# One order table for all engines in the window steps of a two-layer network: layer 0's steps rewritten, with transposes and attention a few steps later

## The chip, the core and the metric

The kernel runs on one core of one Trainium2 chip. The metric is the device time of one execution in microseconds, the median of three runs. The core has five instruction queues that run beside one another and meet at semaphores: TensorE (PE; its weight loads are shown as PEld), VectorE (DVE), ScalarE (ACT), GpSimd (POOL) and SyncE (SP), which here issues all the DMAs. Each queue executes in order: an instruction that waits holds up everything behind it on its own engine.

## The reference, cut to what matters

Sixteen images of 128 channels and 56 x 56 pixels go through two layers. The change is in layer 0 only, so layer 1 (a convolution, a state-space scan over eight tokens, a group norm) is left out here. Layer 0, for each image:

```python
x = x + dwconv3x3(x)                        # "position"
y = layernorm(x)
q, k, v = split(y @ qkv_w + qkv_b)          # 49 windows of 8 x 8 pixels
idx = top_k(mean(q) @ mean(k).T, 4)         # per window: the four windows it attends to
att = softmax(q * SCALE @ k[idx].T)         # 4 heads, 64 queries, 256 keys
o = att @ v[idx]
o = (o + dwconv5x5(v)) @ wo_w + wo_b        # "lepe"
x = x + o
x = x + gelu(layernorm(x) @ w1 + b1) @ w2 + b2
```

## The kernel before: tiles, steps and order

Channels lie on the 128 partitions. An image is seven rows of windows (`NBLK` = 7 blocks of `BLK` = 448 pixels), a row has seven windows (`WIN` = 7), so an image has 49 windows. The program is written image after image; `_chain` (L149) fixes, for each engine, the order in which the program wrote the instructions. So the order of the calls in the source *is* the order of each queue, and nothing else reorders it.

For each image, 49 calls of `step` (L618), then one call of `mlp` (L720). Step t handles window t of image `im`. It also carries two other pipelines in the gaps. One is the last row's output: `collect`, `project_out`, `residual`, and a layer norm `centred`, `squared`, `variance`, `logarithm`, `exponential`, `second`. The other is the next image's input, `nxt`: one row of `position`, a layer norm, `windows` (y and its window sums), `project` and `keep` for q, k and v. Over and above these run the 25 taps a row of the 5 x 5 convolution on DVE (`convolve_on`, L591, with the counts of `TAPS`), and on POOL the 3 x 3 convolution of the image after next or the next one (`beside_to`, L606).

A window goes through these functions:

- `gather` (L418, SP): four DMAs of 64 KB each bring the four chosen windows' keys and values from DRAM into a `sel` buffer, of which there are six. The gathers run `AHEAD` = 5 windows ahead. Every second window also loads its indices into SP's registers (L422).
- `scores` (L435, PE, eight matmuls at L441) into the one bank pair `ps`; `largest` (L445, DVE L447); `exponentials` (L449, ACT L453, two of them), after which `ps` is free for the next window; `inverse` (DVE L459) and `weights` (POOL L463, two multiplications).
- `transpose_values` (PE L471, for two windows at a time) into bank `pvt`, `keep_values` (ACT L478).
- `transpose_weights` (PE L485) into bank `ptt`, `keep_weights` (ACT L491), `attend` (PE L501) into bank `po`.

Bank `g0` serves the two layer norms' `centred` and the three `project`s in turn; `pvt` serves the transposed values, both `variance`s and `project_out`.

In `step`, scores, maximum, exponentials, inverse and weights are all of window t; the weights' transposes are of window t-1, the attention of window t-2 (in column 4 of a row none, in column 5 two). In column 5 the next image's row is squared and its logarithm taken, in column 6 come its exponential and `windows`, ahead of the last window's exponentials. `keep` of k and v writes to DRAM through SP (L390): two DMAs for k in column 1, behind the gather of window 7r+6, and one for v in column 2. Two loads of a later image's halves (L284) follow the gathers of windows 25 and 29.

`mlp` ends the image: it takes the remaining q, k, v of the next image's last row, loads ACT's table for gelu, does the last attentions, routes the next image (`sums`, `route`), issues that image's first five gathers, and runs seven blocks of the MLP, each with a store of `r` (L583). Before the change six of POOL's `beside` operations for the image after next are issued in steps 45 to 48, six more at the start of `mlp`, and the rest up to `LEAD` = 41 during it.

Of the kernel before, what the change touches and what calls it, by code (L numbers as in the profile page):

```python
# [10 lines left out]
F32 = mybir.dt.float32  # L11
# [6 lines left out]
P = 128  # L18
# [191 lines left out]
def layer0(ctx: ExitStack, tc: tile.TileContext, x, t, x1, conv):  # L210
# [117 lines left out]
        else:  # L328
            nc.gpsimd.tensor_add(im["xh"][i], im["xh"][i], held["tap"])  # L329

    def centred(at, im, i):
        held["pc"] = at[:, 0:BLK]
        nc.tensor.matmul(held["pc"], lhsT=centre, rhs=im["xh"][i], start=True, stop=True)

    def squared(n):
        sq = held["sq"] = w1.tile([P, BLK], F32, tag="sq", name=f"sq_{n}")
        nc.scalar.activation(sq, held["pc"], AF.Square)

    def variance(at):
        held["pv"] = at[:, 0:BLK]  # L340
        nc.tensor.matmul(held["pv"], lhsT=mean, rhs=held["sq"], start=True, stop=True)

    def logarithm(n):
        rstd = held["rstd"] = w1.tile([P, BLK], F32, tag="rstd", name=f"rstd_{n}")
        nc.scalar.activation(rstd, held["pv"], AF.Ln, bias=eps)

    def exponential():
        nc.scalar.activation(held["rstd"], held["rstd"], AF.Exp, scale=-0.5)

    def deviation(n):  # L350
        logarithm(n)
        exponential()

    by_row = "c (r w x) -> c w r x"

    def windows(im, i):

        n = f"{im['b']}_{i}"
        y = held["y"] = w1.tile([P, BLK], F32, tag="y1", name=f"y1_{n}")
        nc.vector.tensor_mul(  # L360
            y.rearrange("c (w r x) -> c w r x", w=WIN, r=8),
            held["pc"].rearrange(by_row, r=8, w=WIN),
            held["rstd"].rearrange(by_row, r=8, w=WIN),
        )
        if i == 0:
            im["sum"] = w2.tile([P, NW], F32, tag="ysum", name=f"ysum_{n}")
            im["val"] = w2.tile([P, NW, WP], F32, tag="val", name=f"val_{n}")
            im["dram"] = dram.tile([NW, P, 3, WP], F32, tag="dkv", name=f"dkv_{n}")
        nc.vector.tensor_reduce(
            im["sum"][:, WIN * i : WIN * i + WIN], y.rearrange("c (w p) -> c w p", p=WP), AX.X, ALU.add  # L370
        )
# [186 lines left out]
    def residual(im, r):  # L558
        xh = im["xh"][r]
        nc.vector.scalar_tensor_tensor(xh, held["pw"], wo_b, xh, ALU.add, ALU.add)  # L560

    def second(im, r):
        y2 = im["y2"][r] = w1.tile([P, BLK], F32, tag=f"y2{r}", name=f"y2_{im['b']}_{r}")
        nc.vector.tensor_mul(y2, held["pc"], held["rstd"])

# [16 lines left out]

    TAPS = ((2, 1), (2, 0), (2, 1), (2, 1), (2, 1), (2, 1), (1, 1))

    slot = [0]

# [9 lines left out]

    ROUND = NBLK * len(OPS)
    LEAD, FIRST = 41, 26
    ENDS = (9, 16, 23, 30, 37, 45)
    begun = [ROUND]

    def beside_to(n, count):  # L606
# [8 lines left out]
        scores(im, t)  # L615
        largest(im, t)

    def step(im, nxt, t):  # L618
        r, c = divmod(t, WIN)
        b = im["b"]  # L620
        n = f"{b}_{t}"
        out, row = (im, r - 1) if r else (images[b - 1], NBLK - 1)
        old, new = r > 0 or b > 0, nxt is not None
        if t + AHEAD < NW:
            gather(im, t + AHEAD)
        if t == 0 and early and not new:
            conv.load(0)
        if t in ((20, 24) if b else (30, 34, 38, 42)) and b + 2 < NB:
            load(b + 2, t // 4 - 5) if b else load(2, t // 4 % 2, t // 8 % 2)

        if c < 3 and new and r:
            keep(nxt, r - 1, c)
        if c == 2 and old:
            residual(out, row)
        if c == 3 and old:
            squared(n)
        if c == 6 and new:
            exponential()
        if c == 5 and new:
            squared(n)  # L640
        if t > 0 or b == 0:
            open_step(im, t)
        for w in {4: (), 5: (t - 3, t - 2)}.get(c, (t - 2,)):
            if w >= 0:
                attend(im, w)
        if c == 1 and r:
            collect(im, r - 1)
        if c == 4 and old:
            second(out, row)
        if c == 6 and new:  # L650
            windows(nxt, r)
        taps = TAPS[c] if t else (1, 2)
        convolve_on(taps[0])
        if new:
            lead = LEAD if b else FIRST
            if t in ENDS:
                position(nxt, 1 + ENDS.index(t), (8,))
            if t < 45:
                beside_to(b + 1, lead + -(-(ROUND - lead) * (t + 1) // 45))
            else:  # L660
                beside_to(b + 2, 3 * (t - 44) // 2)
        exponentials(im, t)
        inverse(im, t)
        if t in (3, 10, 17, 31):
            surround(im, 3 + (3, 10, 17, 31).index(t))
        if t in (38, 45) and new:
            surround(nxt, (t - 38) // 7)
        weights(im, t)
        if c == 1 and new and r:
            project(g0, 2)  # L670
        waits = c in (1, 4, 6)
        if not waits:
            piece(im, nxt, out, row, c, r)
        if c == 4:
            transpose_values(im, t)
        if t > 0:
            transpose_weights(im, t - 1)
            if c == 3 and old:
                deviation(n)
            keep_weights(im, t - 1)  # L680
        if c % 2 == 0:
            if c != 4:
                transpose_values(im, t)
            keep_values(im, t)
        if c == 5 and new:
            logarithm(n)
        convolve_on(taps[1])
        if waits:
            piece(im, nxt, out, row, c, r)

    def piece(im, nxt, out, row, c, r):

        old, new = r > 0 or im["b"] > 0, nxt is not None
        if c == 0 and new and r:
            project(g0, 1)
        if c == 1 and old:
            project_out(pvt)
        if early and not new:
            first(r if c > 4 else r - 1, {5: (0, 1, 2), 6: (3, 4), 0: (5, 6, 7), 1: (8,)}.get(c, ()))
        if c == 2 and old:  # L700
            centred(g0, out, row)
        if c == 3 and old:
            variance(pvt)
        if c == 4 and new:
            centred(g0, nxt, r)
        if c == 5 and new:
            variance(pvt)
        if c == 6 and new:
            project(g0, 0)

    early = NB > 2

# [65 lines left out]
    def norm_begun(i):  # L778

        centred((g0, ps[:, 0, :])[i % 2], im, i)  # L780
        means[i] = held["pc"]
        squared(f"0_{i}")


# [27 lines left out]
    begin(im, 4, nc.vector)  # L812
    position(im, 4, (1, 2))
    for i in range(NBLK):
        held["pc"] = means[i]
        windows(im, i)
        if i + 1 < NBLK:
            variance(ptt)
            deviation(f"0_{i + 1}")
# [27 lines left out]
        position(images[1], 0, (8,))  # L847
    for b in range(NB):
        im, nxt = images[b], images[b + 1] if b + 1 < NB else None
        for w in range(NW):  # L850
            step(im, nxt, w)
        mlp(im, nxt)
        if b:
            images[b - 1].clear()
    r = NBLK - 1
    project_out(pvt)
    residual(im, r)
    centred(g0, im, r)
    squared("end")
    variance(pvt)  # L860
    deviation("end")
    second(im, r)
    _act_set(tc, "gelu_and_others")
    for s in range(3):
# [562 lines left out]
```

## Time and profile before

| | us |
|---|---|
| median of three runs | 8227.22 (8224.33 to 8235.01) |
| the profiled execution's own time | 8228.15 |
| its span, first to last instruction | 8226.3 |
| PE busy in the span | 7775.7 (95%) |
| DVE busy | 7590.8 (92%) |
| POOL busy | 6994.9 (85%) |
| ACT busy | 5681.2 (69%) |
| first scores of image 0 | 86.8 |
| last scores of image 15 | 3030.3 |

The granted clock is 0.988 of full speed over the span and 1.00 in the steps of layer 0. The stretch of layer 0 is some 3 of the 8.2 ms; the rest is layer 1, whose instructions the change leaves as they are. An image's cycle, from one image's sixth gather to the next one's, takes 184 to 188 us in images 1 to 13. The 43 windows from window 5 to 48 take 130 to 132 us of it.

How to read it: a row "1098.72:1119.86" is a stretch of the span in microseconds, followed by its length and each engine's busy time in it with the number of instructions. In a list of waits, "DVE y L360 <- ACT rstd L348: 35.4, 87, 0.7" says that DVE's instruction of line 360 stood idle for what ACT did at line 348, 35.4 us in all, 87 times, 0.7 us at the longest. In a timeline the columns are the start, the length from the first to the last of a merged group, the engine, the line, the operation, the tile written from the tiles read, and the count.

### The profile page before, as it was taken

How to read it: one execution, taken by the hardware profiler on the slowest of the kernel's cores; microseconds unless marked ns; L12 is line 12 of the kernel's file. 1: busy time of each engine (PE TensorE's matmuls, PEld its weight loads, DVE VectorE, ACT ScalarE, POOL GpSimd, SP SyncE). 2: the span in 40 equal slices, each digit the busy share in tenths (PEclk: the TensorE clock that was granted, in tenths of full speed). 3: DMA queues.
4: the chain of work that ended last, by engine and by line, in shares of the span. 5: the costliest groups of instructions: out<-in, count | busy, mean ns of one | idle time of the engine just before them, and what ended most of it. 6: DMA issues, size and time to landing. Idle time of an engine off the chain costs nothing.

```text
span 8226.3 us, 155700 instructions
## 1 busy us (share of the span) xinstructions
PE 7775.7 (95%) x53380; PEld 3294.9 (40%) x53380; DVE 7590.8 (92%) x10105; ACT 5681.2 (69%) x10695; POOL 6994.9 (85%) x5569
## 2 busy tenths in 40 slices
PE   8899999999999988999999999999999999999998
PEld 4444444444444443333333333333333333333333
DVE  7999999999999958999999999999999999999998
ACT  5777777777777756666666766666766666666665
POOL 7888888888888627899999998989998989989997
PEclk9999999999999999999999999999999999999998
DMA  5544455554544423333434434333334333344333
GB/s 117 116 111 113 115 115 116 116 118 115 115 112 113 110 75 83 92 89 97 108 82 105 103 88 105 100 90 100 96 90 109 83 103 101 89 104 104 88 92 86
DMA packets 1072005, 835.24 MB, mean 102 GB/s; under 512 B 496112, under 2 KB 971376, under 8 KB 1069296
## 3 DMA queue, kind: packets, MB, share of 16 engines
q1 hardware_dynamic: 1071216, 825.28, 41.0%
q8 instruction: 427, 7.00, 0.4%
q14 instruction: 362, 2.97, 0.1%
HBM read 645.13 MB, written 179.83 MB: 100 GB/s over the span
## 4 chain that ended last, share of the span: by engine, by line
PE 52%; DVE 21%; POOL 11%; ACT 9%; issue 5%; DMA 1%; SPq 0%; DVEq 0%; ACTq 0%; POOLq 0%
PE a L1053 10%; PE pq L185 9%; PE pq L1099 5%; DVE h L1071 5%; POOL xh L329 4%; DVE a L1081 4%; PE x L1064 4%; DVE h L1086 3%; POOL tap L327 3%; PE pq L1133 3%; POOL e L463 2%; PE ptt L485 2%; PE pq L1105 2%; ACT e L453 2%; PE ps L441 2%
## 5 line engine op out<-in xcount | busy, mean ns | idle before, releaser
L1090 POOL TENSOR_TENSOR cst<-h,cb 128x1792 f32<-128x1792 f32 x784 | 3129.3, 3998 | 341.0 <-DVE h L1086 271.5
L1056 ACT ACTIVATE a<-a 128x896 f32<-128x896 f32 x1568 | 1415.9, 903 | 1191.2 <-PE x L1064 969.1
L1071 DVE TENSOR_TENSOR h<-x,bb 128x896 f32<-128x896 f32 x1568 | 1696.3, 1082 | 134.1 <-PE x L1064 100.0
L544 DVE SCALAR_TENSOR_TENSOR lepe<-vpad,lep,lepe 128x448 f32<-128x448 f32 x2688 | 1707.5, 677 | 0.5
L1053 PE MATMUL a<-dt,adec 32*128 32x448 f32 x6272 | 1616.3, 591 | 56.1 <-DVE h L1086 54.5
L1064 PE MATMUL x<-dtx,amask 32*128 32x448 f32 x6272 | 1619.7, 592 | 42.1 <-DVE h L1071 32.5
L1081 DVE TENSOR_TENSOR a<-a,h 128x896 f32<-128x896 f32 x1344 | 1465.2, 1090 | 70.2 <-ACT a L1056 66.7
L1086 DVE TENSOR_TENSOR h<-a,h 128x896 f32<-128x896 f32 x1344 | 1465.1, 1090 | 42.0
L463 POOL TENSOR_SCALAR e<-e,sst,zero 128x256 f32<-128x256 f32 x1568 | 855.4, 555 | 528.5 <-DVE sst L459 446.0
L453 ACT ACTIVATE e<-ps,sst 128x256 f32<-128x256 f32 x1568 | 726.8, 468 | 456.0 <-DVE sst L447 417.7
L1053 PEld LDWEIGHTS a<-dt,adec 32*128 32x128 f32 x6272 | 473.1, 184 | 1063.7 <-issue 295.2
L329 POOL TENSOR_TENSOR xh<-xh,tap 128x448 f32<-128x448 f32 x742 | 845.7, 1140 | 33.3
L185 PE MATMUL pq<-pad,conv 128*128 128x448 f32 x1890 | 836.2, 560 | 0.0
L1099 PE MATMUL pq<-cst,sel 128*32 128x448 f32 x6272 | 731.0, 551 | 0.5 <-POOL cst L1090 0.5
L447 DVE TENSOR_REDUCE sst<-ps 128x2 f32<-128x512 f32 x784 | 540.0, 689 | 100.9 <-PE ps L441 68.4
L146 ACT ACT_TABLE_LOAD x484 | 621.0, 1283 | 9.2 <-PEq L1418 0.7
L1064 PEld LDWEIGHTS x<-dtx,amask 32*128 32x128 f32 x6272 | 473.7, 184 | 320.4 <-DVE h L1071 296.6
L485 PE MATMUL ptt<-ident,e 128*128 128x128 f32 x3136 | 506.5, 280 | 86.5 <-POOL e L463 43.0
L441 PE MATMUL ps<-sel,q 32*64 32x256 f32 x6272 | 522.2, 402 | 36.2 <-ACT e L453 17.1
L485 PEld LDWEIGHTS ptt<-ident,e 128*128 128x128 f32 x3136 | 370.0, 141 | 382.8 <-issue 189.3
L491 ACT COPY att<-ptt 128x512 f32<-128x512 f32 x784 | 455.6, 581 | 81.7 <-PE ptt L485 81.3
L185 PEld LDWEIGHTS pq<-pad,conv 128*128 128x128 f32 x1890 | 324.6, 189 | 358.4 <-issue 350.7
(185 smaller groups left out, 12202.5 us busy)
## 6 DMA issues: line engine op xcount, KB each, us to landing
sel<-dkv SPq DMA_DIRECT2D x3136, 64.0 KB
bb<-db SPq DMA_DIRECT2D x336, 448.0 KB
cb<-dc SPq DMA_DIRECT2D x336, 448.0 KB
dkv<-key SPq DMA_DIRECT2D x224, 224.0 KB
dkv<-val SPq DMA_DIRECT2D x112, 224.0 KB
x<-r SPq DMA_DIRECT2D x112, 224.0 KB
pad<-x SPq DMA_DIRECT2D x16, 1568.0 KB
db<-bs SPq DMA_DIRECT2D x112, 224.0 KB
```

The lines of the kernel that those rows point to most:

```text
L185: self.nc.tensor.matmul(bank[:, 0:BLK], lhsT=self.weights[:, k, :], rhs=self.pad[:, 8 * i + dy : 8 * i + dy + 8, dx : dx + W], start=(k == ...
L329: nc.gpsimd.tensor_add(im["xh"][i], im["xh"][i], held["tap"])
L485: nc.tensor.transpose(ptt[:, P * (2 * p + h) : P * (2 * p + h + 1)], e[:, h * P : (h + 1) * P], ident)
L544: nc.vector.scalar_tensor_tensor(out, src, lep[:, k : k + 1], acc, ALU.mult, ALU.add)
L1053: nc.tensor.matmul(a[:, k, :], lhsT=adec[rows, l4, :], rhs=p["dt"][rows, h, :], start=True, stop=True)
L1056: nc.scalar.activation(p["a", l, jp], p["a", l, jp], AF.Exp)
L1064: nc.tensor.matmul(x[:, k, :], lhsT=mask[rows, l4, :], rhs=p["dtx"][rows, h, :], start=True, stop=True)
L1071: nc.vector.tensor_mul(p["h", l][:, own(jp), :], px["x"], weight)
L1081: nc.vector.tensor_mul(a, a, before)
L1086: nc.vector.tensor_add(h, p["a", l, jp], h)
L1090: nc.gpsimd.tensor_mul(c, p["h", l], p["gate", 1, l].unsqueeze(1).to_broadcast([P, 4, BLK]))
L1099: nc.tensor.matmul(py[32 * j : 32 * j + 32], lhsT=sel[:, l4, :], rhs=p["c", l][:, j, :], start=False, stop=(l % 4 == 3), skip_group_check= ...
```

## The change

`step` and `piece` are gone, and `TAPS` and `ENDS` with them. In their place stands `ORDER`, 124 tokens that give the order of one row of seven windows. A token is a function's name and a column: `scores:3` is the fourth window of the row. A column may be negative or above 6 and then means a window of the row before or after: `keep_weights:-2` belongs to the sixth window of the row before, `gather:11` to the fifth of the next. Tokens without a column are fillers: `tap` (one tap of DVE's convolution, 19 a row as before), `beside` (POOL, ten a row) and `surround`. The pieces of the two layer norms have columns too: `windows:-7` is the next image's row whose logarithm was taken at the end of the last row. `windows_of` walks the table nine times for an image and calls what the token names; tokens that fall outside the image's windows are skipped, and a few are left to `mlp`.

What moves, read from the table: before, the weights of window t were transposed behind the scores of t+1; now those of a row's first three windows stand behind the scores of t+2, the others as before. Attention to window t, before behind the scores of t+2 (in one column t+3), now stands behind those of t+3 (in two columns t+2). The values of a pair of windows, before transposed in the step of the first of them, are now transposed behind the scores of the second. Output and input pieces no longer share a column with a step; the next image's `exp_in`, `windows` and `project_q` follow in the next row. `window_sums` is split off `windows`. The two layer norms keep separate entries in `held` (keys "o" and "n"); their tiles have the same tags and buffers as before. The `beside` operations up to all 105 of the next image are spread over the first 58 tokens of an image, and the last twelve tokens issue one operation each for the image after it, so twelve instead of six precede `mlp`.

```diff
-    TAPS = ((2, 1), (2, 0), (2, 1), (2, 1), (2, 1), (2, 1), (1, 1))
+    ORDER = """
+        scores:0 tap weights:-1 exp_in:-7 transpose_values:-1 maximum:0 keep_weights:-2 beside
+        windows:-7 gather:5 exponentials:0 transpose_weights:-1 tap project_q:-7 beside keep_values:-1
+        tap scores:1 keep_weights:-1 inverse:0 tap weights:0 keep_q:-7 attend:-2 maximum:1 attend:-1
+        project_k:-7 window_sums:-7 beside exponentials:1 tap transpose_values:0 collect:0 keep_k:-7
+        scores:2 beside gather:6 tap keep_values:0 transpose_weights:0 beside maximum:2 project_v:-7
+        inverse:1 tap exponentials:2 project_out:0 weights:1 position:0 gather:7 keep_weights:0 scores:3
+        inverse:2 residual:0 beside keep_v:-7 attend:0 maximum:3 transpose_weights:1 beside tap
+        centre_out:0 exponentials:3 tap transpose_values:2 weights:2 keep_weights:1 tap scores:4
+        gather:8 keep_values:2 inverse:3 tap transpose_weights:2 beside square_out:0 maximum:4 attend:1
+        keep_weights:2 variance_out:0 weights:3 tap exponentials:4 tap transpose_weights:3 surround
+        gather:9 log_out:0 tap scores:5 inverse:4 exp_out:0 attend:2 weights:4 maximum:5
+        transpose_values:4 keep_weights:3 second:0 exponentials:5 transpose_weights:4 beside tap
+        centre_in:0 gather:10 tap keep_weights:4 scores:6 keep_values:4 inverse:5 tap weights:5
+        square_in:0 attend:3 maximum:6 attend:4 variance_in:0 tap beside exponentials:6 gather:11 tap
+        transpose_weights:5 log_in:0 inverse:6
+    """.split()
...
-    ENDS = (9, 16, 23, 30, 37, 45)
...
-    def step(im, nxt, t):
...
+    BESIDE, BY_ROW = 58, ORDER.count("beside")
+
+    def filler(im, nxt, name, r, k):
+
         b = im["b"]
...
+        if name == "tap":
+            convolve_on(1)
+        elif name == "surround":
+            i = (3, 4, 5, None, 6, 0, 1)[r]
+            if i is not None and (i > 1 or nxt):
+                surround(im if i > 1 else nxt, i)
+        elif nxt:
+            lead, n = LEAD if b else FIRST, BY_ROW * r + k
+            if n <= BESIDE:
+                beside_to(b + 1, lead + -(-(ROUND - lead) * n // BESIDE))
+            else:
+                beside_to(b + 2, n - BESIDE)
...
+        elif name == "gather":
+            gather(im, t)
+            if im["b"] + 2 < NB:
+                if im["b"] == 0 and t in (35, 39, 43, 47):
+                    load(2, (t - 35) // 4 % 2, (t - 35) // 8)
+                elif im["b"] and t in (25, 29):
+                    load(im["b"] + 2, (t - 25) // 4)
...
+    FIRST_TAPS = {"variance_in": (0, 1, 2), "project_q": (3, 4), "project_k": (5, 6, 7), "project_v": (8,)}
+    LAST = {("transpose_weights", NW - 1), ("keep_weights", NW - 1), ("attend", NW - 2), ("attend", NW - 1)}
+
+    def windows_of(im, nxt):
+
+        b = im["b"]
+        for q in range(-1, NBLK + 2):
+            fillers = {}
+            for token in ORDER:
+                name, _, c = token.partition(":")
+                if not c:
+                    if 0 <= q < NBLK:
+                        k = fillers[name] = fillers.get(name, 0) + 1
+                        filler(im, nxt, name, q, k)
+                    continue
+                t = WIN * q + int(c)
+                r = t // WIN
+                if not 0 <= t < NW:
+                    continue
+                if name in OUTPUT:
+                    if r:
+                        of_output(im, r - 1, name)
+                    elif b and name != "collect":
+                        of_output(images[b - 1], NBLK - 1, name)
+                elif name in INPUT:
+                    at_end = r == NBLK - 1 and name in ("project_k", "keep_k", "project_v", "keep_v", "keep_q")
+                    if nxt and not at_end:
+                        of_input(nxt, r, name)
+                    elif early and not nxt and name in FIRST_TAPS and not (r == NBLK - 1 and at_end):
+                        first(r, FIRST_TAPS[name])
+                elif name == "gather":
+                    if t >= AHEAD:
+                        of_window(im, name, t)
+                elif (name, t) not in LAST and (t or not b or name not in ("scores", "maximum")):
+                    of_window(im, name, t)
+                    if (name, t) == ("exponentials", 0) and early and not nxt:
+                        conv.load(0)
...
-        for w in range(NW):
-            step(im, nxt, w)
+        windows_of(im, nxt)
         mlp(im, nxt)
```

`of_output` and `of_input`, left out here, call for each of their names the function that `step` and `piece` called before: `centre_out` is `centred(g0, ...)`, `variance_out` and `variance_in` are `variance(pvt)`, `log_*` and `exp_*` are `logarithm` and `exponential`, `project_q` is `project(g0, 0)`.

For the last image there is no next one; `first` then computes layer 1's first convolution on PE in the places of `variance_in` and the `project`s, as before in the corresponding columns.

## The prediction

> **What bounds the kernel now.** The change touches the window steps of layer 0 (the first 3030 us). I read the stretches of single rows first, then the waits of the steady part, then SP's queue through one whole image.
>
> One row of seven steps, by stretches (stretch, length, then busy time and count of PE, PEld, DVE, ACT, POOL, clock, DMA share, GB/s):
>
> ```profile
> 1098.72:1119.86 21.14, 19.46 (x226) 10.46 (x226) 20.03 (x39) 17.16 (x49) 17.59 (x29) 1.00 0.79 144
> 1119.86:1141.09 21.23, 19.69 (x227) 10.52 (x228) 20.06 (x40) 17.22 (x49) 17.22 (x28) 1.00 0.47 114
> ```
>
> A row takes 21.1 to 21.2 us, of which DVE is busy 20.0 and PE 19.5: no engine is free, none is full, at the full clock. What DVE and PE wait for, 300 to 2600 us (12.5 images, some 87 rows):
>
> ```profile
> DVE y L360 <- ACT rstd L348: 35.4, 87, 0.7
> DVE xh L560 <- PE pvt L556: 27.9, 79, 1.0
> DVE sst L447 <- PE ps L441: 25.2, 84, 1.7
> ...
> PE ps L441 <- DMA sel<-dkv: 5.6, 6, 1.6
> ```
>
> DVE's three waits come to 88.5 us, about 1 us a row; that is what a better order can win. DMA releases the scores only six times, for 5.6 us. That looks harmless, so I asked how close it is. SP's queue in image 5 (start, length, what, count of DMAs), the image's last scores, and the first gather of the next image's steps:
>
> ```profile
> 1019.00 23.06 SPq L428 DMA_DIRECT2D sel<-dkv  x36
> ...
> 1098.01 14.92 SPq L428 DMA_DIRECT2D sel<-dkv  x20
> ...
> 1117.99 16.29 SPq L428 DMA_DIRECT2D sel<-dkv  x24
> ...
> 1139.89 16.44 SPq L428 DMA_DIRECT2D sel<-dkv  x24
> ```
>
> ```profile
> 1160.41 0.66 PE L441 MATMUL ps<-sel,q 32*64 32x256 f32 x8
> ```
>
> ```profile
> 1202.85 5.01 SPq L428 DMA_DIRECT2D sel<-dkv  x8
> ```
>
> The gathers stand shoulder to shoulder: 24 of them in 16.4 us is 2.74 us a window. Counting the row's three dkv writes (1.0 and 0.4 us) and the waits at a full queue, SP needs, in the median of images 1 to 13, 20.5 us for seven windows in windows 5 to 25, 25.9 us for the six windows behind the two image loads (25 to 31), and 21.1 us for seven after that. In image 5 only 2.4 us of its 135 us from gather 5 to gather 48 are waits for a semaphore. I matched every gather with its landing and its scores. In image 5 the time from landing to scores is 8.1 us at window 5, 11.0 at window 25, 1.0 at window 30, and 2.5 at window 48. In images 1 to 13 its least value lies between 0.1 and 2.4 us. So **SP's queue is nearly as critical as the engines, in the second half of each image.**
>
> Three numbers of the trace then make the image's cycle. From gather 5's issue to gather 48's landing: 136.8 to 141.6 us, mean 139.3 (images 1 to 13). From gather 5 to the last scores: 141.4 to 145.7, mean 142.7. From the last scores to the next image's gather 5 (tail, MLP, last store): 42.4 to 42.5 us in twelve of these thirteen images and 42.8 in one, a fixed chain.
>
> **The row in the new order.** Every instruction of the row is still there: 19 taps, 7 maxima, 8 products of 448 columns, 7 x 4 gathers. The work is the same, so only waits can change. I walked the table by hand, each start being the later of engine free and producer done, with the shortest start-to-start steps of these rows. They are: scores to maximum 0.79 us, maximum to exponentials 0.73, exponentials to the next scores 1.0 and to the inverse 1.06, inverse to weights 0.26, weights 1.07. Further: transposes to their copy 0.69, copy to attention 0.65, a 448-column product to its reader 1.0 and to the next matmul 0.86; a tap 0.59, a maximum 0.60. From DVE's first tap the maxima start at 0.59, 3.69, 6.53, 9.23, 12.26, 14.83, 17.95 and the next row's first at 20.62: **20.05 us a row**. DVE stalls in three places only: 0.13 at maximum:5 (scores:5 waits for exponentials:4), 0.2 at maximum:6 (scores:6 stands behind centre_in), and 0.2 at the next maximum:0 (scores behind transpose_weights:5). The old waits go: windows stands a row later than log_in and exp_in, residual 1 us behind project_out. So 1.1 us less a row, if gathers are there.
>
> POOL: ten beside tokens a row issue 64 operations over 58 tokens, 11.0 a row against 10.0 before. At 0.93 us each (products 0.79, sums 1.11, begin 0.70) that is 10.3, plus seven weights of 1.07 and the surround of 0.95: 18.7 of 20.05 us. Where a token issues two, weights:2 and :3 come up to 0.9 late; the row may then be 20.4. In image 0 (79 operations) POOL's sum is 21.1, so there the row gains about 0.6.
>
> Twelve beside operations instead of six precede the MLP. The six cost POOL 6 us less in the MLP, but the 42.4 us chain holds PE and ACT, not POOL: nothing.
>
> Gathers: their order is the same; the two key writes move ahead of gather 7r+6. SP is behind by then and finds the key copied: nothing, up to 0.4 us in the first rows. A sel buffer is freed by the value transposes, which now lag: gather:8 can go 11.4 us ahead of its scores, gather:11 12.4 us. Before, window 25's went 14.3 us ahead (image 5). With scores 25 some 3 to 4 us earlier that does not bind; at 20.6 us a row it would.
>
> **The images.** Images 1 to 13 are paced by SP: with gathers landing as now and 0.14 us a window to catch up, each image's last scores can come earlier by the least slack left, 0.6 to 3.9 us, mean 1.9, sum 24. SP's own waits that vanish give perhaps 0.5 each, 6.5 (an estimate from the 2.4 us above; from 0 to 2).
>
> The **tail** gets longer. Before, log and exp of the next image's row 6 stood ahead of the last exponentials, and y was done 1.9 us after the last scores; gelu began after 5.58 us (1160.41 to 1165.99). Now variance_in stands behind scores:6 and two attentions on PE (1.42 us), log_in behind exponentials:6 on ACT (2.45), then exp_in (3.13), y (3.74), project_q (4.41), keep_q (5.47), the table load (6.1) and gelu at 7.4. Behind them wait, on PE, attend 47, both expands, transpose_weights 48 and project_k, all of the fixed chain. So +1.8 us for 15 images: +27.
>
> Images 0, 14 and 15 are not paced by SP (least lead 4.8, 5.7, 12.6 us late in the image). Image 0: six rows by 0.6, 3.5. Image 14: six rows by 1.0, 6. Image 15 has no next image: its row is 24.6 us, PE busy 22.6, DVE idle a quarter. With convolution taps spread over four places it may come to 23.1: 9 us in six rows (from 0 to 12).
>
> Sum: -24 - 6.5 + 27 - 3.5 - 6 - 9 = **-22 us**. The profiled execution took 8228.15 us (span 8226.3 and 1.9 around it), 0.9 above the median of 8227.22. So 8206 on its scale, 8205 on the median's.
>
> A rule that speaks against this: the Trainium skill, "DMA: Bandwidth & Descriptors", section "Issuing engines are not separate DMA queues", calls the sequencer's time to start a DMA "usually small relative to the DMA itself". Here four gathers take 2.1 us of SP and land 1.9 us after the last (median), so the row denies it. By the rule nothing would be charged to SP and the change would be worth what the second case below says.
>
> **The rivals.** *The engines' saving arrives whole:* SP is pushed less than I think, because its blocked issues (17 us an image) shrink. Then 0.8 us by 6.1 rows, plus 1.4 us in the lighter row 0, less 1.8 of tail, is 4.5 us an image: 15 x 4.5 + 9 = 76, 8150. For it: POOL and PE have room for 20.3 us. Against: 21.1 us per seven windows on SP after the loads.
>
> *Slower, by the tail:* the sel buffers, held longer, delay the gathers, so SP's run from gather 5 to 48 lengthens by the 1.9 us that I count as won. It decides once the new row is above 20.6 us, or once the run exceeds 141.5 us. Then the last scores come as before, the tail's 27 us stay, and image 15 gives 4: about 8250. For it: the shorter reach of 11.4 us. Against: SP was hardly ever held by a buffer.
>
> That the row is not reordered can't be: the table fixes every engine's order.
>
> **How the numbers follow.** My forecast 0.52, 8185 to 8227; the whole saving 0.20, 8130 to 8185; slower by the tail 0.28, 8225 to 8270. About 0.2% (16 us) is what a measurement here tells from no change: 8211 to 8243 counts as the same. Of the forecast two thirds lie below 8211 (0.34), the rest within; all of the second case is faster; of the third 0.22 is slower. Faster 0.54, same 0.24, slower 0.22. The range reaches into both rivals: 8150 to 8255.
>
> **What would show it.** Right: rows 1 to 3 take about 20.1 us; in images 1 to 13 the landing-to-scores time falls to 0.2 us at most windows from 30 on, and DMA as the scores' releaser grows from 5.6 us to over 50; the last scores to the next gather 5 take 44.2 us. Wrong: SP's run falls well below 137 us (the whole saving), rows above 20.6 us, a tail of 42.4 us still, or image 15 unmoved.

## The result, and the profile after

The changed kernel takes **8284.78 us** (median of six runs, 8280.31 to 8294.95) against 8228.38 for the kernel before on the same chip: ratio 1.007, 95% interval 1.0057 to 1.0083. It is slower by 56 us. The prediction was 8205, with a range from 8150 to 8255: the result lies above the range, and the kernel became slower where it was to become faster. The profiled execution took 8286.06 us (span 8284.3), 1.3 above the median. All of the loss lies in layer 0: the last scores of image 15 come at 3087.2 us instead of 3030.3.

First the rows, image 5, rows 1 to 4 by stretches (columns as in the prediction: length, busy time and count of PE, PEld, DVE, ACT, POOL, then clock, DMA share, GB/s):

```profile
1061.52:1081.80 20.28, 19.24 (x227) 10.29 (x226) 19.63 (x41) 16.87 (x49) 18.75 (x28) 1.00 0.50 122
1081.80:1102.14 20.34, 19.25 (x227) 10.28 (x226) 19.63 (x41) 16.86 (x49) 19.17 (x29) 1.00 0.49 121
1102.14:1122.72 20.58, 19.19 (x227) 10.33 (x227) 20.03 (x42) 17.26 (x49) 18.63 (x27) 1.00 0.76 134
1122.72:1143.50 20.78, 16.02 (x170) 8.57 (x170) 14.59 (x30) 12.37 (x36) 13.41 (x21) 0.92 0.75 136
```

Rows 1 and 2 take 20.3 us where a row took 21.1 to 21.2: the new order does what it says. In the fourth stretch PE is idle for 23% of the time and DVE for 30%, and the row does not even end in it. Something else has taken over. The waits of 300 to 2600 us, the same view as in the prediction, say what:

```profile
DVE sst L450 <- PE ps L444: 122.0, 118, 5.5
...
PE ps L444 <- DMA sel<-dkv: 61.0, 23, 5.3
...
DVE xh L563 <- PE pvt L559: 21.7, 23, 1.9
...
DVE y L360 <- ACT rstd_6n L348: 11.6, 12, 1.0
```

The waits that the change was to remove are smaller (xh 27.9 to 21.7, y 35.4 to 11.6). But the scores now wait 61 us for gathers, and the maxima 122 us for scores (25.2 before). SP's queue in image 5, from the timeline, shows where the gathers lost their time:

```profile
1042.46 23.87 SPq L431 DMA_DIRECT2D sel<-dkv  x32
1067.64 1.01 SPq L393 DMA_DIRECT2D dkv<-key  x2
...
1107.77 4.48 SPq L431 DMA_DIRECT2D sel<-dkv  x4
...
1125.41 11.69 SPq L431 DMA_DIRECT2D sel<-dkv  x16
```

The first 32 gathers take 23.87 us; before, 36 of them took 23.06. The key write that followed gather 13 now stands ahead of it. Gathers 5 to 25 take SP 62.3 us on average of images 1 to 13 (58.8 before), of which 5.0 are gaps, that is, waits of SP of over 0.5 us each (1.1 before). SP runs ahead of the scores, and this lead shrinks: from the landing of gather 25 to its scores it is 4.6 us on average of the same images (10.4 before). SP's own waits, before and then after, 300 to 2600 us:

```profile
SPq L390 <- ACT key L388: 129.7, 12, 13.2
...
SPq L428 <- PE pvt L471: 24.8, 45, 2.6
```

```profile
SPq L393 <- ACT key L391: 168.7, 31, 13.4
...
SPq L431 <- PE pvt L474: 45.1, 54, 3.5
SPq L431 <- PE po L504: 35.1, 42, 4.0
```

Twelve of the waits for the key are the image's last key write, in the MLP, in both kernels. The other nineteen are new, and so is the growth at the value transposes (`pvt`, from 24.8 us) and at `po` (from 18.1). There a gather waits until PE has read the `sel` buffer that it is to overwrite. Only the scores and the value transposes read `sel`; the view names the PE instruction nearest to the release, so `po` is taken for such a wait too.

The image's end, from the timeline (last scores, y, table load, first gelu) and SP's next gathers:

```profile
1187.59 0.66 PE L444 MATMUL ps<-sel,q 32*64 32x256 f32 x8 [0.60 <-DMA sel<-dkv]
...
1191.28 0.62 DVE L360 TENSOR_TENSOR y<-g,rstd_6n 128x448 f32<-128x448 f32 x1 [0.97 <-ACT rstd_6n L348]
...
1193.67 1.28 ACT L146 ACT_TABLE_LOAD   x1
...
1194.97 0.63 ACT L578 ACTIVATE hid<-ps,bias 128x448 f32<-128x448 f32 x1
```

```profile
1231.84 8.04 SPq L431 DMA_DIRECT2D sel<-dkv  x11
```

Gelu begins 7.38 us after the last scores (5.58 before), and the next image's sixth gather, at 1231.84, 44.25 after them (42.44).

The image's cycle, means of images 1 to 13, in us. "Run" is from gather 5's issue to gather 48's landing, "steps" from gather 5's issue to the last scores, "tail" from there to the next gather 5:

| | run | steps | tail | cycle | image 0 | image 14 | image 15, steps |
|---|---|---|---|---|---|---|---|
| before | 139.4 | 142.7 | 42.4 | 185.1 | 179.8 | 183.8 | 162.0 |
| after | 144.1 | 145.2 | 44.4 | 189.5 | 185.3 | 181.7 | 159.2 |

Thirteen cycles by 4.4 are 57 us; image 0 adds 5.5, images 14 and 15 give back 4.9.

### The profile page after: what moved, and what is told of

The parts are those of the page before. It is cut to its first block, busy times and chain, and to the rows that moved or that the text cites. A ratio compares the mean times of both kernels' runs of the same rounds, so it can differ in the third digit from the quotient of the medians.

```text
span 8284.3 us, 156477 instructions
## 1 busy us (share of the span) xinstructions
PE 7807.2 (94%) x53380; PEld 3305.0 (40%) x53380; DVE 7566.6 (91%) x10105; ACT 5652.2 (68%) x10695; POOL 7029.1 (85%) x5569
## 4 chain that ended last, share of the span: by engine, by line
PE 55%; DVE 25%; POOL 8%; ACT 5%; issue 5%; DMA 1%; SPq 1%; POOLq 0%; DVEq 0%; ACTq 0%
PE a L1116 10%; PE pq L185 9%; PE pq L1162 6%; DVE h L1134 5%; DVE lepe L547 4%; PE x L1127 4%; DVE a L1144 4%; DVE h L1149 3%; POOL e L466 3%; DVE sst L450 3%; PE pq L1196 3%; PE ps L444 2%; PE pq L1168 2%; POOL xh L329 2%; PE po L583 2%
## 5 line engine op out<-in xcount | busy, mean ns | idle before, releaser
L466 POOL TENSOR_SCALAR e<-e,sst,zero 128x256 f32<-128x256 f32 x1568 | 890.3, 578 | 450.4 <-DVE sst L462 298.3
L488 PE MATMUL ptt<-ident,e 128*128 128x128 f32 x3136 | 534.7, 290 | 75.5 <-ACT att L494 51.3
```

What stands on the lines that cost most here:

```text
L466: nc.gpsimd.tensor_scalar(e, e, im["st", w][:, 2, p : p + 1], zero, ALU.mult, ALU.add)
```

## The experiments

The theory to test (**SP theory**): images 1 to 13 are paced by SP's gathers; the row is faster, but SP is held by key writes and buffers that the new order frees later, and what is lost there is not made up behind the image loads. Three rivals: the **engine rival** (the order is itself slower on PE, DVE and ACT), the **clock rival** (what costs is that the matmul clock now drops, see the last section) and the **tail rival** (the 1.8 us at the image's end are all). Times are medians; the ratio is to the kernel before on the same chip. The lines of an edited kernel lie up to 8 further down. The edits are shown cut to the lines that matter, some of them in outline.

### Who sets the pace: the loads on another queue, and no loads at all

```diff
 def load(b, two, half=None):
-    nc.sync.dma_start(pads[b % 2][...], xv[b, two][...])
+    nc.scalar.dma_start(pads[b % 2][...], xv[b, two][...])
```

On the changed kernel:

> The changed kernel with the loads of image b+2 issued from ACT's queue instead of SP's. SP theory (the changed kernel's images 1 to 13 are paced by SP's gathers, and what SP has lost is time held at buffers and key copies): the two loads no longer stand between the gathers of windows 25 and 31, which take 25.9 us for six windows instead of about 18, so gather 5 to gather 48's landing falls from 144.2 to about 137 us and gather 5 to the last scores from 145.1 to 138 or 139 (image 14, which has no loads, takes 137.5): 13 images by 6, so about 8207 us, 8190 to 8225. Engine rival (the new order is itself slower on DVE, PE and ACT): no change within 0.2%, or slower by what ACT pays to issue the loads. Clock rival (only the drops of the matmul clock cost): the drop at windows 30 and 31 goes, the one in row 0 stays, about 20 us less. Tail rival (only the 1.8 us behind the last scores): no change.

On the kernel before:

> The kernel before with the same edit, as a control. SP theory: SP was barely the bound there; image 14, without loads, took 141.4 us from gather 5 to the last scores against 142.7 in images 1 to 13, so 1.3 us by 13 images, about 17 us less: 8211, 8195 to 8230; and the gap between this kernel and the changed one with the same edit closes from 56 to under 10 us. Engine rival: no change in either, and the gap stays 56. Clock rival: no change here (the kernel before has hardly any drops), gap 36. Tail rival: no change, gap 56.

Measured: 8323.65 (1.0116, 1.0099 to 1.0133) and 8323.82 (1.0113, 1.0096 to 1.0129). Both are far slower, and by no theory's number. SP's waits in the edited changed kernel, and its DMA share (last but one) in 5 us of image 5:

```profile
SPq L431 <- DMA pad<-x: 46.6, 6, 8.7
SPq L431 <- DMA y<-x: 43.6, 6, 8.7
```

```profile
1115.00:1120.00 5.00, 4.33 (x58) 2.35 (x54) 4.94 (x11) 4.29 (x14) 4.82 (x8) 1.00 1.32 154
```

In twelve places SP now waits for the *landing* of a load that it did not issue, up to 8.7 us: in the trace, gather 23's last DMA waits on semaphore 108, which a load on ACT's queue counts as well. So the edit put a new wait in place of the one it removed. The two kernels come out equal, 92 us above the kernel before and 39 above the changed one, but that decides nothing: these waits are not the same in the two (90.2 us in the changed kernel, 128.6 in the kernel before, in twelve places each, from 300 to 2600 us). The loads' transfers fill the DMA engines whoever starts them: in the changed kernel, where SP starts them, the DMA share comes to 1.34 from 1110 to 1115 us. The cleaner experiment leaves the loads out:

```diff
-    elif im["b"] and t in (25, 29):
-        load(im["b"] + 2, (t - 25) // 4)
```

> The changed kernel without the image loads in images 1 to 13; it computes images 3 to 15 from the data that images 1 and 2 left in the two pads, so only its time is of use. SP theory: the six windows behind the loads take SP 18 us instead of 25.5, so images 1 to 13 become like image 14 (137.4 us from gather 5 to the last scores, against 145.2): 13 by 7.8, 101 us less, 8184, 8165 to 8205. Engine rival: the loads are nothing to PE, DVE and ACT, so within 0.2% of 8285. Clock rival: about 20 less. Tail rival: no change.

> The kernel before without the image loads in images 1 to 13, with the same part left out. SP theory: images 1 to 13 like its image 14 (141.4 against 142.7): 13 by 1.3, 17 us less, 8211, 8200 to 8225. So without the loads the changed kernel is the faster one of the two by 15 to 40 us, where with them it is slower by 56. Engine rival: no change, and the changed kernel stays slower by 56 in this pair too.

Measured: **8192.33** for the changed kernel (0.9946, 0.9929 to 0.9963) and **8221.46** for the kernel before (0.9984, 0.9974 to 0.9993). Without the loads the changed kernel is the faster one by 29 us; with them it is slower by 56. Steps: 137.7 against 142.2 us. The changed kernel's waits for gathers are nearly gone (61.0 us before the edit):

```profile
DVE sst L450 <- PE ps L444: 58.7, 111, 1.2
...
PE ps L444 <- DMA sel<-dkv: 3.9, 8, 1.1
```

This ends the engine rival: PE, DVE and ACT do the same work in the same order as in the changed kernel, and are 4.5 us an image ahead of the old order. It also ends the tail rival (the tail is 44.2 here too) and the clock rival, which gave 20 us: it got 92. SP's gaps in gathers 5 to 25 stay without the loads (62.0 us for these gathers, 62.3 with them), and cost little there: what the loads take is what the lead is missing for.

### What holds SP: buffers, key writes, both

```diff
-    w6 = tile_pool(name="l0w6", bufs=AHEAD + 1)
+    w6 = tile_pool(name="l0w6", bufs=AHEAD + 3)
```

> The changed kernel with eight sel buffers instead of six, so that no gather waits for a buffer that a value transpose still holds. SP theory: SP's waits for pvt and po transposes and attentions (45 and 18 us in 12.5 images) vanish, and gather 5 to gather 48's landing falls by 2 to 4 us in images 1 to 13: about 8245 us, 8230 to 8260. Engine rival, clock rival and tail rival: within 0.2% of 8285.

```diff
-  scores:2 beside gather:6 tap                 # keep_k:-7 ahead of it also writes
+  scores:2 beside gather:6 write_key:-7 tap    # keep_k:-7 only copies
```

> The changed kernel with the two DMAs that write a row's keys put back behind gather 7r+6 on SP, where they stood before the change; ACT's copy of the key stays where the change put it. SP theory: SP's wait for ACT's key copy (168.7 us in 31 places of 12.5 images, against 129.7 in 12; twelve of each are the images' first, at 10.8 to 12 us, so some 25 to 35 us lie inside the images) goes for the greater part: 1 to 2 us an image, about 8265 us, 8255 to 8275. Engine, clock and tail rivals: within 0.2% of 8285.

Measured: 8297.28 (1.0082, 1.0065 to 1.0099) and 8280.14 (1.0058, 1.0041 to 1.0074). Alone, the buffers give nothing and the key writes some 5 us, which is within the noise: two misses. (The 18 us that the first expectation gives for `po` are the kernel before's; the changed kernel has 35.1.) SP in image 5 of the kernel with eight buffers:

```profile
1039.72 20.58 SPq L431 DMA_DIRECT2D sel<-dkv  x32
1064.22 1.01 SPq L393 DMA_DIRECT2D dkv<-key  x2
```

The 32 gathers now go out in 20.58 us instead of 23.87. Then SP stands still from 1060.30 to 1064.22, because the key is not copied yet. The wait did not go, it moved. Both at once:

> The changed kernel with both edits at once: eight sel buffers, and the key writes back behind gather 7r+6. In the run with eight buffers alone, SP ran up to the key write in front of gather 13 and waited 3.84 us there (image 5); in the run with the key alone, the waits for the buffers' value transposes grew from 45 to 65 us. SP theory, sharpened: each hold takes up what the other lets go, so only both together raise the time from landing to scores ahead of the image loads (window 25: 5.7 us in the changed kernel, then about 9); SP's gaps in gathers 5 to 25 fall from 5 to about 1 us, and gather 5 to the last scores from 145.2 to about 139.5 in images 1 to 13, 74 us in all: 8211, 8190 to 8235. Engine rival and tail rival: within 0.2% of 8285, as each edit alone. Clock rival: the drop at windows 30 and 31 goes, at most 20 us: 8265.

Measured: 8263.30 (1.0037, 1.0023 to 1.0051); steps 143.2, SP's gaps in gathers 5 to 25 1.6 us instead of 5.0. So the two edits together give 21 us, where alone they gave 5 and nothing, but that is a third of what I expected. 13 waits for the key (1.2 us each) were left, one gather on. Nine buffers, with both writes later still:

```diff
-  gather:8 keep_values:2 ...       gather:9 log_out:0 ...
+  gather:8 write_k:-7 keep_values:2 ...       gather:9 write_v:-7 log_out:0 ...
```

> The changed kernel with nine sel buffers, the key writes of a row behind gather 7r+8 and its value write behind gather 7r+9 of SP's queue. With eight buffers and the key behind 7r+6, 13 waits of 1.2 us for ACT's key copy and a wait before gather 14 were left, and gather 5 to the last scores came to 143.2. SP theory: no write waits for a copy any more, the time from landing to scores at window 25 rises from 7 to about 11 us, of which the loads take 8.3, so that images 1 to 13 are no longer paced: 138 to 139 us from gather 5 to the last scores instead of 145.2, 80 to 93 us in all: 8198, 8180 to 8225. If SP's own work is the bound (57 to 58 us of issue for gathers 5 to 25, 26 behind the loads, 51 to the end, 2 to land), not its waits: 141 us, 8230. Engine and tail rivals: 8285.

Measured: **8231.77** (1.0001, 0.9991 to 1.0011), steps 140.9, the run 139.7, gaps 1.0, the lead at window 25 8.6 us. The expectation's second branch, "SP's own work is the bound": it gave 141 and 8230. From the changed kernel this takes away 53 of the 56 us with no change in the engines' order, so the holds on SP, together with the loads, were the loss. Its image 5:

```profile
1023.01 28.61 SPq L439 DMA_DIRECT2D sel<-dkv  x44
...
1097.98 4.88 SPq L383 DMA_DIRECT2D dkv<-key  x2
```

Eleven windows go out in one piece (2.6 us a window). Behind the second load (1097.25) the key writes take 4.88 us instead of 1.00: there the issue itself takes SP longer.

### Row 0, the tail, and everything together

Row 0's edit: the inverse of window 0 and the maximum of window 1 ahead of taps.

```diff
-  tap scores:1 keep_weights:-1 inverse:0 tap weights:0 ... maximum:1 attend:-1
+  scores:1 keep_weights:-1 inverse:0 tap weights:0 ... maximum:1 attend:-1 tap tap
```

> The changed kernel with the first row of each image reordered: the inverse of window 0 and the maximum of window 1 ahead of three of the taps, two of which follow behind that maximum. (The run with four edits had one tap too many there in each image, so its later images were computed with shifted convolution work.) SP theory: scores 0 to 5 take 16 us instead of 17.8, and the matmul clock's drop in row 0 goes; but in images 1 to 13 SP's queue takes most of it back, so 5 to 20 us less: 8272, 8260 to 8283. Clock rival: the drop costs what the row lost, so 1.8 us in 15 images, 27 less, 8258 or lower.

Measured: 8275.23 (1.0049, 1.0032 to 1.0066). Scores 0 to 5 take 16.5 us instead of 17.8, the steps 144.0 instead of 145.2: 10 us in all, within the SP theory's numbers. The clock's drop did not go with it (27 drops in images 1 to 14, 28 before the edit), so that half of the expectation failed.

One kernel put four edits together. Its last row had the input's variance, log and exp ahead of the last exponentials. Its first row held one tap too many in each image, so that the convolution of the later images is shifted.

> The changed kernel with four edits: eight sel buffers, key writes behind gather 7r+6, the first row of an image with its first two windows' maxima ahead of three taps again, and in the last row the input's variance, log and exp ahead of the last exponentials again. SP theory: 139 us from gather 5 to the last scores instead of 145.2 in images 1 to 13, the tail 42.5 instead of 44.3 in all images, and the matmul clock's drop in row 0 gone: 81 + 27 + 4 = 112 us less, 8173, 8150 to 8205, faster than the kernel before. Engine rival: only the tail and row 0 give something, 25 to 55 us: 8230 to 8260. Clock rival: both drops go and the tail, 65 us: 8220. Tail rival: 27 us, 8258.

Measured: 8273.24 (1.0045, 1.0028 to 1.0062), a miss: the tail was 44.8 us, not 42.5. Log and exp ahead of the exponentials pushed these back, the inverse behind them stood ahead of y on DVE, and y came 4.3 us after the last scores instead of 3.7. Another edit of the tail swaps the two layer norms of the last row:

```diff
+  LATE = ORDER with centre_in:0 ... exp_in:0 windows:0 project_q:0 keep_q:0 in the places of
+         centre_out:0 ... second:0, and centre_out:0 ... log_out:0 in theirs
```

> The changed kernel with the two chains of an image's last row swapped: the next image's row 6 (centre, variance, log, exp, y, query) takes the earlier places, the output of row 5 the later ones, so the table load ahead of the MLP waits for the output's exp instead of y, the query product and its copy. Expected: from the last scores to the next gather 5 about 42 us instead of 44.3, in 15 images: 35 us less, 8250, 8238 to 8262. Tail rival: the same, and with it the greater part of the 57 us. SP theory: the same here, and gather 5 to the last scores stays at 145.

Measured: 8283.88 (1.0061, 1.0045 to 1.0078). The tail is 43.9, a gain of 0.5 instead of 2.3; the steps were 146.1. The last exponentials now stand behind the output's square on ACT, and its exp still precedes the table load. So neither edit won the tail back: with log and exp behind the last exponentials the chain ends later, and ahead of them they push the exponentials back.

> The late writes with nine buffers, the reordered first row and the swapped last row together. SP theory: 138 to 139 less about 1.8 of row 0, which now arrives as SP no longer paces: 137 us from gather 5 to the last scores, a tail of 42: 13 by 8 and 15 by 2.3, and 4 of images 0 and 14, some 140 us less than the changed kernel: 8145, 8120 to 8180, faster than the kernel before by 0.6 to 1.3%. If SP's own issue is the bound: 141 and 42, 8195. Engine rival: the tail and row 0 alone, 8225.

Measured: 8225.83 (0.9991, 0.9981 to 1.0000), no measurable change from the kernel before. The run is 139.7 again, the steps 141.0, although row 0 is 1.5 us shorter. With few holds left, SP's run sets the same bound, and what the engines win is lost in waiting for it. What is open now is what these 139.7 us are: SP's own issues, or the transfers.

### Issues or transfers: the key and value writes from ACT's queue

```diff
 def write(im, i, s):
-    nc.sync.dma_start(im["dram"][...], kept)
+    nc.scalar.dma_start(im["dram"][...], kept)
```

All transfers stay; SP loses three issues a row.

> The changed kernel with the three DMAs that write a row's keys and values issued from ACT's queue, behind gathers 7r+7 and 7r+8 in the order, where ACT has made the copies long before; six sel buffers as in the changed kernel, all gathers on SP. SP-issue theory: SP loses three issues of 0.4 us and their waits in each row, so gather 5 to gather 48's landing falls from 144.1 to 134 to 136 us and gather 5 to the last scores from 145.2 to 138 (the engines' own time, 137.5): 13 images by 7, 90 less, 8195, 8180 to 8225. Transfer theory (the DMA engines' time for the loads, the gathers and the writes is the bound, whoever issues): 139.5 us at the least, as in the run with late writes, and the buffers' waits stay: 8250 to 8285. Engine rival: 8285, or slower by what the issues cost ACT.

> The same with nine sel buffers and the reordered first row. SP-issue theory: no wait is left on SP, its run of 131 to 134 us is below the engines' 136, and row 0's 1.4 us arrives: gather 5 to the last scores 136 to 137, 13 by 8.5 and 5 of images 0 and 14, some 115 us less than the changed kernel: 8170, 8150 to 8200. Transfer theory: no better than the run with late writes, 8220 to 8232.

> The same with the last row's two chains swapped too, which gave 0.5 us in the tail (44.37 to 43.9) before: 7 us less than the run before it, 8163, 8143 to 8195, on either theory 7 less than that one.

> Control: the kernel before with its key and value writes issued from ACT's queue, directly behind the copies. SP-issue theory: its engines need 141.4 (image 14) to 142.2 (the run without loads) from gather 5 to the last scores, against 142.7: at most 6 to 17 us less, 8218, 8205 to 8232, so that the changed kernel's order with the same edit is then the faster one by some 20 to 50 us. Transfer theory and engine rival: 8231, no change, or slower by ACT's waits for its own copies (0.2 us each, up to 3 an image).

Measured:

| | time | ratio (95%) | run | steps | tail |
|---|---|---|---|---|---|
| changed, writes on ACT | 8242.40 | 1.0014 (1.0005 to 1.0024) | 136.5 | 141.9 | 44.5 |
| and nine buffers, row 0 | 8196.44 | 0.9962 (0.9948 to 0.9976) | 132.1 | 137.3 | 44.3 |
| and the swapped tail | 8189.77 | 0.9952 (0.9936 to 0.9969) | 132.6 | 137.9 | 44.0 |
| before, writes on ACT | 8321.23 | 1.0108 (1.0092 to 1.0125) | 144.2 | 149.3 | 42.4 |

The run falls from 139.7 to 132 us with every transfer still made, so what set the 139.7 was SP's issues; the transfers alone allow 132 or less. The closest pair is the last kernel of the section above (8225.83, run 139.7) and the third variant (8189.77, run 132.6): they differ only in the queue of the writes and in their place, one gather earlier. The first variant alone missed its 8195: with six buffers SP still waits 98.8 us for value transposes. SP in image 5 of the second variant, and its scores' waits for gathers:

```profile
1013.84 55.51 SPq L439 DMA_DIRECT2D sel<-dkv  x84
1069.45 1.90 SPq L284 DMA_DIRECT2D y<-x  x1
1072.20 16.36 SPq L439 DMA_DIRECT2D sel<-dkv  x16
```

```profile
PE ps L452 <- DMA sel<-dkv: 6.0, 5, 1.8
```

21 windows in one unbroken piece of 55.51 us are 18.5 us a row, below the engines' 20.1 to 20.3; what the load then takes (16.36 us for four windows) the lead pays for. This is **the same engine order as the changed kernel's, row 0 apart, and faster than the kernel before** (which has neither the nine buffers nor the moved writes); the last variant, 8189.77, is the best seen, within the error of the second.

The control missed: the kernel before with that edit is 91 us slower. Its SP waits for the other queue's writes to land:

```profile
SPq L428 <- DMA dkv<-key: 133.1, 87, 4.6
```

That is the wait of the first pair of runs again (40.0 us in 18 places in the second variant, where the writes stand later). So it says nothing of how much the kernel before could win from fewer issues on SP. The nearest to that is the kernel before without its loads, which won 15 us.

## Why the prediction was wrong, point by point

- **The row, 20.05 us: right.** 20.3 in rows 1 and 2; from scores 5 to 25 of image 5, where no gather is late, 57.4 us, 20.1 a row. Image 14, which has no loads, did its 43 windows in 124.7 us instead of 129.9. Its term in the sum, -6, came to -3.9 in the steps, row 0 included.
- **The tail, +1.8: right.** 44.25 against 42.44 in image 5, and 1.7 to 1.9 more in fourteen of the fifteen images (3.3 in one). The steps by which it was worked out are those of the timeline (y +3.69 against 3.74, gelu +7.38 against 7.4).
- **"SP's queue is nearly as critical as the engines": right,** and too mild. DMA as the scores' releaser rose to 61 us, as the text wanted over 50; in every one of images 1 to 13 there are windows behind the loads whose scores follow the landing by 0.1 to 0.2 us. But they are one to six an image, not most windows from 30 on as I had it (9% there are under 0.25 us, half under 2 us): one late gather delays the steps enough for the next few to be early.
- **"SP is behind by then and finds the key copied: nothing, up to 0.4 us in the first rows": the step that failed first.** In image 5 SP reached the write ahead of gather 13 1.2 us too early, and 3.84 us too early once it had buffers enough. No row stands behind the bound of 0.4; before, the write stood one gather on, and the view puts none of SP's waits inside the steps down to the key's copy. SP is not behind in the early rows: there it is ahead, and is to build up the lead that the loads then consume.
- **"With scores 25 some 3 to 4 us earlier that does not bind": the step that failed with it.** A buffer freed later by the transposes held gather 8 for 2.78 us in image 5. I asked whether the reach of 11.4 us is enough for gather 25, and not what it does to gathers 8 to 14, whose lead is needed 15 windows later. The two together are the 4.3 us by which the late writes with nine buffers shorten the steps (145.2 to 140.9); the prediction's own figure was 140.3. This one term is 13 by 4.9, 64 of the 79 us between forecast and result. How the 4.3 us divide between the buffers, the key writes and the value write was not shown.
- **Row 0 was not walked.** Taken as 1.4 us lighter, and that only in a rival, it became 1.1 us later (scores 0 to 5: 16.7 to 17.8).
- **Image 0, -3.5 predicted, and +3.7 besides the tail's 1.8.** The prediction's own sum for POOL, 21.1 us a row there, was above its walked row, and I still booked a gain. From scores 5 to 48 POOL is busy 124.5 of 136.2 us (117.4 of 135.0 before). PE's weight loads wait longer for POOL's weights; that this is the cause was not tested. Before and after:

```profile
PEld ptt L485 <- POOL e L463: 10.7, 24, 1.4
```

```profile
PEld ptt L488 <- POOL e L466: 25.8, 46, 1.9
```

- **Image 15, -9 predicted, -2.8 measured.** Its 43 windows gained 4.6, of which row 0 took back part. What else keeps the row above the 23.1 us I gave it was not tested.
- **The rivals.** The third, slower, had the right direction and the right mechanism (buffers held longer lengthen SP's run by more than is won; it decides above 141.5, measured 144.1), but lacked the key write, so its 8250 was too low. I gave it 0.28 against the argument "SP was hardly ever held by a buffer", a finding about the old order. The second, the saving arriving whole, comes nearest in the kernels without loads: 29 us between them, not the 76 it asked for.

What stays open: why the clock's drop outlives the edit of row 0; why the steps of image 14 take 2 us more in the last two variants than in the changed kernel, although its gathers land 6.6 us or more ahead of their scores; and what the old order would win from the same writes on ACT's queue without the new waits.

## What to carry to other kernels

Where a queue of transfers runs nearly as tight as the engines, its lead is a stock: ask of each moved instruction where the stock is built and where it is spent, not whether the transfer is late where it stands. A wait that is hardly there before says nothing about an order that moves what releases it; and of several holds in a row on one queue, lifting one only carries the queue to the next, so lift all of them before judging. Where a queue's issues are the limit, give some to another queue, but look for waits between the two.

## What the runs showed of the hardware

**The matmul clock halves after a short idle.** In the stretches of image 5's row 0 the granted clock (third from the end) reads:

```profile
1038.00:1044.20 6.20, 4.38 (x27) 1.89 (x26) 5.15 (x10) 1.02 (x4) 3.56 (x5) 1.00 0.26 90
1044.20:1046.00 1.80, 0.00 (x0) 0.00 (x0) 1.80 (x4) 1.02 (x5) 1.80 (x4) 0.50 0.35 92
1046.00:1051.00 5.00, 4.95 (x34) 2.15 (x38) 2.35 (x7) 1.97 (x6) 4.03 (x6) 0.50 0.41 105
1051.00:1056.00 5.00, 5.00 (x64) 3.09 (x59) 5.00 (x10) 4.16 (x13) 4.48 (x9) 1.00 0.21 53
```

PE had waited 3.39 us for window 1's exponentials, and its eight score matmuls then took 1.13 us instead of 0.66:

```profile
1046.05 1.13 PE L444 MATMUL ps<-sel,q 32*64 32x256 f32 x8 [3.39 <-ACT e L456]
```

From the first scores of image 1 to gather 5 of image 15 the clock is at half speed for 143 us in 28 stretches of 3.4 or 6.8 us; before it was 17 us in 4. The Trainium skill, "TensorE: Matmul & The Clock Gate", section "Part 1: The HAM clock gate", puts both the idle time that lowers the clock and the busy time that raises it at about 3.4 us, and calls the window free-running. The trace agrees in the lengths of the stretches. In the idle time it does not, if that means idle without a break: here PE was busy until 1042.66, and at 1044.20, after 1.5 us, the clock had fallen. The page's section "HAM oscillation — how this bites in real kernels" tells of a kernel that pays it at each wait for a DMA. Here the drops at windows 30 and 31 come with such waits, but the kernel without loads kept 15 drops (65 us) and was the faster one all the same.

**Two queues that share semaphores wait for each other.** A load moved to ACT's queue cost SP up to 8.7 us at a gather of the changed kernel, a write up to 4.6 us in the kernel before. The loads cost ACT next to nothing: an issue took it 0.6 us, and its next activation began 0.13 us after the one before had ended (median of 24). The Trainium skill, "DMA: Bandwidth & Descriptors", section "Issuing engines are not separate DMA queues", says that all queues' transfers interleave on the same 16 engines and that a second queue saves the sequencer's time alone. The first half agrees with the loads on ACT's queue, behind which the DMA share rose to 1.32, as it did to 1.34 with the loads on SP's. As to the second, the sequencer's time, which it calls usually small, was here some 7 us of an image's 140 (the run's 139.7 against 132.6).
